# A selective scan with convolution and attention on one core: preparation of steps re-timed, image ends allowed to run over, and a wide last end

## The chip, the cores and the metric

The kernel runs on one core of one Trainium2 chip. The metric is the device time of one execution in microseconds (us). A profiled execution gives a trace of every instruction on each engine: PE (TensorE matmul; PEld is its weight load), DVE (VectorE), ACT (ScalarE), POOL (GpSimd) and SP (SyncE, which here only issues DMAs).

## The reference

The input x is 8 images of 64×64 positions × 96 channels, fp32. Two layers follow, cut here to what matters:

```python
# layer 0:  x = x + ss2d(groupnorm(x))
xh, z = split(x @ in_proj_w.T)                    # 192 + 192 channels
xc = silu(depthwise_conv3x3(xh) + conv_b)
s0, s1 = xc[diag], xc[anti]                       # two walks over the 4096 positions
xs = [s0, s1, s0[::-1], s1[::-1]]                 # four directions
dts, Bs, Cs = split(x_proj_weight @ xs)           # 6 + 16 + 16 rows
delta = softplus(dt_projs_weight @ dts + bias)
h_t = h_{t-1} * exp(delta_t * A) + (delta_t * u_t) * B_t     # per channel and state, 16 states
y_t = sum over states of h_t * C_t;  ys = y + D * xs
y = the four directions put back in place and added
out = (layernorm(y) * ln_w + ln_b) * silu(z) @ out_proj_w.T
# layer 1:  t = t + linear_attention(layernorm(t)) (6 heads);  t = t + ffn(layernorm(t))
# the ffn has 96 -> 384 -> 96 channels, inputs and weights rounded to 5+2 bits, sums to 5+10 bits
```

## The kernel before

**The main loop.** An image is scanned in 16 steps: two passes q (forward directions, then backward), each of 8 chunks of T=512 positions. The two directions of a pass lie together on the 128 partitions, in G=3 groups of channels. Each step has 16 states n, so there are 128 steps m and 2048 iterations i = 16·m + n in `run`. One iteration issues, in this order:

- `decay(i+2)`: three Exp on ACT (L966), from delta;
- `times_b(i+2)`: where FEED[n] is "A", eight scaled copies on ACT (L980) into feedT, from duT and rows. FEED is "DADADADADADAAAAA": n=0, 2, 4, 6, 8 and 10 go the other way, by one pick matmul (L990) and three DVE multiplies (L1005) in `recur`;
- `recur(i)`: three scans on DVE (L1001), of 512 elements each;
- `turn(i+1)`: PE transposes (L988) of feedT into the three feed banks of PSUM;
- `reduce(i-4)`: PE transposes (L1036) of the products into the y banks, where the 16 states are summed;
- `keep(i-1)` and `read(i-1)`: on POOL the carry (L1017) and the product of h and C (L1022);
- `fetch(i+4)`: two DMAs on SP that broadcast a row of C into cc.

PSUM's eight banks are three of feed, three of y and two ("bank") shared by everything else.

**The preparation of a step** is `prologue(m+2)`, started at n=13 of step m. It makes x_proj (L878), rows (L883), their transposes (L888) and x (L891); |dt| in three groups (matmul L901, ACT Abs L903), Exp (L905) and Ln (L908); then four passes on POOL (L912, L913, L915, L917), which together give log(1+e) with a correction of its rounding; then delta in three groups (matmul L920, DVE L922), du on POOL (L929), its transposes (L934) and copies into duT on ACT (L936). `bring(m+2)`, at n=8, loads u, and first finishes side work until that chunk has been walked.

**Side work** is everything that isn't the loop: `measures` (group norm statistics), `front` (norm, convolution L536, silu, image stores L562, and the walk: loads of ut on SP L581, transposes L588), and `tail` (`join` from L614: normalises y, gates it, projects it; `attention`; `layers`: attention's output and the FFN). It is written as generators. Class `Work` advances them in fixed places of an iteration, by a credit of us for each place ("P" for PE three times an iteration, "A" for ACT, "V" for DVE, "G" for POOL). Urgent jobs (prologues) come first. In its alone mode, `finish(enough)`, it runs whatever is there until a condition holds. [...]

During image b, `between(b)` runs the front of image b+1 and then the tail of image b-1. The hand-over is at iteration LAG+1 = 5 of an image:

```python
            if at == LAG + 1 and b:
                work.finish(all_done)
                work.stream(between(b))
```

The measures of image b+2 start in mid-image. Before the loop, image 0's front runs until two chunks are walked, and prologue(0) is finished together with whatever side work is there. After the loop, `end(7)`, the last tail, runs with the feed banks freed, three chunks at a time. The join of a chunk stores t (`at.mid`) and the transposed xaT (`at.turned`) to DRAM, and `layers` loads them.

Of the kernel before, what the change touches and what calls it, by code (L numbers as in the profile page):

```python
# [50 lines left out]
@with_exitstack  # L51
def hybrid_block(ctx, tc, x, out, w):


    nc = tc.nc
    NB = x.shape[0]
    const = ctx.enter_context(tc.tile_pool(name="const", bufs=1))
    dram = ctx.enter_context(tc.tile_pool(name="dram", bufs=4, space=DRAM))
    k = weights(tc, const, dram, w)
    pool = ctx.enter_context(tc.tile_pool(name="scan", bufs=1))  # L60
    psum = ctx.enter_context(tc.tile_pool(name="psum", bufs=1, space=PSUM))
    with tc.manual_schedule():

        k.tables = lambda: nc.scalar.preload_act_table_set("natural_log_exp_and_others")
        run(tc, pool, psum, dram, x, out, k, NB)


def weights(tc, const, dram, w):
# [60 lines left out]
    logs = tile("logs", [P, ND, NJ])  # L129
    turned = tile("turned", [ND * NJ, P])  # L130

    def loads():

        nc.sync.dma_start(out=logs, in_=w["a_logs"])
        for d in range(2):
            for g, a, lo, hi, at in PIECES:
                rows = slice(d * GC + at, d * GC + at + hi - lo)
                for first, n, name in ((0, NR, "w_dt"), (XB, NS, "w_b"), (XC, NS, "w_c")):
                    nc.sync.dma_start(
                        out=k.wx[rows, :, g, first + d * n : first + (d + 1) * n], in_=w[name][lo:hi, a, d::2, :]  # L140
                    )
                nc.sync.dma_start(out=dd[rows, :, g], in_=w["ds"][lo:hi, a, d::2])
                for q in range(2):
                    bias = w["b_step"][lo:hi, 2 * q + d, a : a + 1].rearrange("i o -> o i")
                    nc.sync.dma_start(out=k.ws[2 * NR : 2 * NR + 1, q, g, rows], in_=bias)
                if g:
                    yield SPIN
            for q in range(2):
                nc.sync.dma_start(
                    out=k.ws[d * NR : (d + 1) * NR, q, :, d * GC : (d + 1) * GC],  # L150
                    in_=w["w_step"][:, 2 * q + d, :].rearrange("r (g i) -> r g i", i=GC),
                )


        ps = yield bank(0.2, 3)
        v = view(ps, ND * NJ, P)
        nc.tensor.transpose(v, logs.rearrange("p k j -> p (k j)"), k.ident)
        yield act(0.4)
        nc.scalar.copy(turned, v)
        k.release(ps)  # L160
        rows = dram.tile([ND * NJ, P], F32, tag="logs", name="logs")
        nc.sync.dma_start(out=rows, in_=turned)
        yield SPIN
        for q in range(2):
            for d in range(2):
                for g in range(G):
                    j = (2 * q + d) * NJ + g * (GC // DPT)
                    nc.sync.dma_start(
                        out=k.a_neg[d * GC : (d + 1) * GC, q, g, :],
                        in_=rows[j : j + GC // DPT, :].rearrange("j (i n) -> (j i) n", n=NS),  # L170
                    )
            yield SPIN
# [18 lines left out]
    def layers():  # L191
# [18 lines left out]
        with tc.tile_pool(name="prep", bufs=1, side="right") as prep:  # L210
            w1s = load("w1s", [DM, HID], w["w1"], pool=prep)
            w2s = load("w2s", [P, 3, DM], w["w2"], pool=prep)
            b1s = load("b1s", [P, 3], w["b1"], pool=prep)
            b2s = tile("b2s", [P, 4, DM], pool=prep)
            nc.sync.dma_start(out=b2s, in_=w["b2"].unsqueeze(1).to_broadcast([P, 4, DM]))
            for _ in range(2):
                yield SPIN

            nc.vector.tensor_copy(k.w1q, w1s, saturate=False)
            nc.vector.tensor_copy(k.w2q, w2s, saturate=False)  # L220
            s8 = tile("b1e", [P, 3], F8, prep)
            nc.vector.tensor_copy(s8, b1s, saturate=False)
            nc.vector.tensor_copy(k.b1q, s8)
            s8 = tile("b2e", [P, 4, DM], F8, prep)
            nc.vector.tensor_copy(s8, b2s, saturate=False)
            nc.vector.tensor_copy(k.b2q, s8)
# [38 lines left out]
class Work:  # L265
# [6 lines left out]
    def __init__(self, banks):  # L272
        self.now = 0
        self.alone = False
        self.urgent, self.jobs, self.streams = [], [], []
        self.free = [(b, -9) for b in banks]
        self.kept = []
        self.long = []
        self.credit = dict.fromkeys(self.PLACES, 0.0)
# [40 lines left out]
    def at(self, tag, place=0):  # L320
        gain, most = self.PLACES[tag]
        self.credit[tag] = min(most, self.credit[tag] + gain)
        for j in self.urgent + self.jobs:
            while not j.done and j.tag == tag:
                if j.ready > (self.now, place) and (j.spin or not self.alone):
                    break
                if not self.alone:
                    if self.credit[tag] <= (0.0 if j not in self.urgent else -1.5 if tag == "P" else -99.0):
                        break
                given = None  # L330
                if j.bank:
                    given = self.bank_for(j, place)
                    if given is None:
                        break
                self.credit[tag] -= j.us
                self.proceed(j, given, place)
# [41 lines left out]


# [29 lines left out]
def fetched(nc, pool, x, b, c):  # L409
    xt = pool.tile([P, 4, DM], F32, tag="xt", name="xt", bufs=2)  # L410
# [57 lines left out]
def front(tc, work, x, k, at, b):  # L468
# [8 lines left out]
    with tc.tile_pool(name=f"f1_{b}", bufs=1, **area) as p1, tc.tile_pool(name=f"f2_{b}", bufs=2, **area) as p2:  # L477
# [17 lines left out]
        def norm(c):  # L495

            xt = fetched(nc, p2, x, b, c)
# [104 lines left out]
def tail(tc, work, x, out, k, at, b):  # L602
# [3 lines left out]
    with tc.tile_pool(name=f"t1_{b}", bufs=1, **area) as p1:  # L606
# [3 lines left out]
        with tc.tile_pool(name=f"t2_{b}", bufs=2, **area) as p2:  # L610
# [3 lines left out]
            def join(c):  # L614
                s = slice(4 * c, 4 * c + 4)

                def tile(name, shape, bufs=2):
                    return p2.tile(shape, F32, tag=name, name=name, bufs=bufs)
# [7 lines left out]
                t = tile("t", [P, 4, DM], 3)  # L626
                nc.sync.dma_start(out=t, in_=x[b].rearrange("(t p) c -> p t c", p=P)[:, s, :])
                yield "P", 0.0, 4, False
                while c >= 2 and c - 2 not in joined:
                    yield SPIN  # L630
                gate = tile("gate", [HC, 2, CH])
                nc.sync.dma_start(out=gate, in_=at.gate[:, :, c * CH : (c + 1) * CH])
                st, mv = tile("st", [P, 4, 6]), tile("mv", [P, 4, 2])
                yn = ys[0]
                for j in range(2):
# [21 lines left out]
                yg = tile("yg", [HC, 2, CH])  # L657
# [26 lines left out]
                nc.sync.dma_start(out=at.mid[:, s, :], in_=t)  # L684
# [28 lines left out]
                xaT = ys[1].rearrange("p a c -> p (a c)")[0 : DM + 1, 0:CH]  # L713
# [3 lines left out]
                nc.sync.dma_start(out=at.turned[:, c * CH : (c + 1) * CH], in_=xaT)  # L717
                joined.add(c)

            yield [join(c) for c in range(NCH)], 3  # L720
# [3 lines left out]
        def attention():  # L724
# [14 lines left out]
            kf = yield from small([DM, DM], "kf", vk, k.w_ff)  # L739
# [11 lines left out]
        with tc.tile_pool(name=f"t3_{b}", bufs=3, **area) as p2:  # L751

            def layers(c):
# [5 lines left out]
                xaT = tile("xaT", [DM + 1, CH])  # L759
                nc.sync.dma_start(out=xaT, in_=at.turned[:, c * CH : (c + 1) * CH])  # L760
                t = tile("t", [P, 4, DM])
                nc.sync.dma_start(out=t, in_=at.mid[:, s, :])
# [59 lines left out]
            yield [layers(c) for c in range(NCH)], 3  # L822


def run(tc, pool, psum, dram, x, out, w, NB):
# [9 lines left out]
    nc = tc.nc  # L835
    steps = [
# [26 lines left out]
    def prologue(m):  # L863
# [8 lines left out]
        ps = yield bank(1.0, 0)  # L872
        v = view(ps, P, TB, NX)
        for j in range(TB):
            if j == 2:
                yield pe(0.8)
# [5 lines left out]
        rows = o.rows = tile("rows", [P, TB, NX])  # L882
# [28 lines left out]
        yield gp(3.0)  # L911
        nc.gpsimd.tensor_scalar(f, e, 1.0, 1.0, ALU.mult, ALU.add)  # L912
        nc.gpsimd.tensor_scalar(f, f, -1.0, 1.0, ALU.add, ALU.mult)  # L913
        yield gp(3.4, 1)
        nc.gpsimd.tensor_tensor(e, e, f, ALU.subtract)  # L915
        yield gp(3.4, 1)
        nc.gpsimd.tensor_tensor(delta, delta, e, ALU.add)  # L917
        for g in range(G):
            ps = yield bank(0.85)
# [3 lines left out]
            work.release(ps)  # L923
        o.delta = delta
        yield gp(3.4)
# [4 lines left out]
        for j in range(G):  # L930
            ps = yield bank(0.45)
# [6 lines left out]
        o.duT = duT  # L938
# [85 lines left out]
    def reduce(i, part):  # L1024
# [15 lines left out]
        if q and n in (1, 2, 3) and part == 2:  # L1040
            for j in range(4 * (n - 1), 4 * n):
# [4 lines left out]
                )  # L1046
        if q and n in (8, 9, 10) and part == 2:
# [4 lines left out]
            )  # L1052
        if part == 2:
            hs.pop(i)
# [34 lines left out]

    def between(b):  # L1090
# [5 lines left out]
    def first():  # L1096
# [5 lines left out]
        yield from between(0)  # L1102
# [20 lines left out]
    work.finish(lambda: not work.urgent)  # L1123
# [6 lines left out]
    for tag, at in (("P", 2), ("A", 0), ("P", 2)):  # L1130
        work.now += tag == "A"
        work.at(tag, at)
# [11 lines left out]
    for i in range(total + LAG + 1):  # L1144
        m, n = divmod(i, NS)
        b, at = divmod(i, PER)
        if i < total:
            if at == LAG + 1 and b:
                work.finish(all_done)
                work.stream(between(b))  # L1150
            if at == PER // 2 and b + 2 < NB:
                work.stream(before(b + 2))
            if n == NS - 3 and m + 2 < len(steps):
# [4 lines left out]
        if i + 2 < total:  # L1158
            decay(i + 2)
        work.at("A")  # L1160
        if i + 2 < total:
            times_b(i + 2)
# [19 lines left out]
    work.free += [(f, -9) for f in feed]  # L1182
    work.kept = []
    work.stream(end(NB - 1))
# [78 lines left out]
```

## Time and profile before

| | us |
|---|---|
| median of 3 runs | 12009.75 (12005.47 to 12027.36) |
| the profiled execution | 12015.44 |
| its span | 12013.6, mean granted TensorE clock 0.907 |
| first scan begins | 308.2 |
| last scan ends | 11627.8 |

| of the span | busy us | share |
|---|---|---|
| PE | 9964.7 | 83% |
| DVE | 9683.0 | 81% |
| ACT | 9500.1 | 79% |
| POOL | 9739.2 | 81% |

The largest groups are POOL's product L1022 (7073.5 us, 3454 ns each), DVE's scans L1001 (6502.6 us, 1261 ns), ACT's decays L966 (3976.2 us, 713 ns), PE's transposes L1036 (3806.0 us) and L988 (2746.2 us), and ACT's feedT L980 (3671.1 us, 443 ns). A share of busy time is an average over stages with different limits: the steps with side work beside them take up to 102 us, those without 75.2.

### The profile page before, as it was taken

The page shows a single profiled execution, that of the slowest core. Times are in us where ns is not written, and L with a number is a line of the kernel's source. Part 1 is how long each engine was busy: PE and PEld are TensorE (multiplying, and loading weights), DVE is VectorE, ACT ScalarE, POOL GpSimd, SP SyncE. Part 2 cuts the span into 40 slices and gives each one's busy share as a digit, 9 for nine tenths or more (in the row PEclk, how much of TensorE's full clock was granted, in tenths as well). Part 3 has the DMA queues.
Part 4 walks back from the last instruction along what each step waited for, and adds up shares of the span by engine and source line. Part 5 has one row for each costly group of instructions (what it writes and reads, how often), then busy time and mean ns, then how long its engine had stood idle before and what let it go on. Part 6 is the DMA issues. An engine that isn't in the chain of part 4 may idle for free.

```text
span 12013.6 us, 186895 instructions
## 1 busy us (share of the span) xinstructions
PE 9964.7 (83%) x62805; PEld 8013.1 (67%) x62805; DVE 9683.0 (81%) x11092; ACT 9500.1 (79%) x19843; POOL 9739.2 (81%) x6927
## 2 busy tenths in 40 slices
PE   5888889888898888888898888988889888888875
PEld 4676677666676667766676666766667666666653
DVE  1888988888888888888888888888888878888971
ACT  2888888878887788887888778887788878878862
POOL 0879988889878888788988888878898888889972
PEclk8999999998999989999899999989899998988985
DMA  3234333533335333343334433343333533322331
GB/s 98 84 97 129 100 91 89 136 106 101 88 96 143 98 93 95 107 125 103 91 92 128 116 93 90 95 129 109 96 92 92 134 105 94 105 83 82 99 96 39
DMA packets 1126629, 1213.55 MB, mean 101 GB/s; under 512 B 453061, under 2 KB 732326, under 8 KB 1125670
## 3 DMA queue, kind: packets, MB, share of 16 engines
q1 hardware_dynamic: 1125670, 1201.61, 36.4%
q8 instruction: 499, 8.18, 0.3%
q14 instruction: 460, 3.77, 0.1%
HBM read 877.99 MB, written 323.14 MB: 100 GB/s over the span
## 4 chain that ended last, share of the span: by engine, by line
PE 30%; ACT 20%; DVE 20%; POOL 12%; issue 9%; DMA 4%; SPq 3%; DVEq 0%; POOLq 0%; ACTq 0%
DVE h L1001 13%; ACT feedT L980 8%; PE y L1036 7%; PE feed L988 7%; POOL h L1022 7%; ACT decay L966 6%; DVE feed L1005 4%; PE bank L536 3%; DMA cc<-crow 2%; PE bank L878 2%; SPq L581 2%; POOL delta L917 1%; PE bank L920 1%; PE feed L990 1%; PE bank L901 1%
## 5 line engine op out<-in xcount | busy, mean ns | idle before, releaser
L1022 POOL TENSOR_TENSOR h<-h,cc 128x1536 f32<-128x1536 f32 x2048 | 7073.5, 3454 | 390.0 <-DMA cc<-crow 197.1
L1001 DVE TENSOR_TENSOR_SCAN h<-decay,carry,feed 128x512 f32<-128x512 f32 x5376 | 6502.6, 1261 | 635.1 <-PE feed L988 528.8
L966 ACT ACTIVATE decay<-delta,a_neg 128x512 f32<-128x512 f32 x6144 | 3976.2, 713 | 1287.5 <-DVE h L1001 1281.8
L988 PE MATMUL feed<-ident,feedT 128*128 128x128 f32 x15360 | 2746.2, 303 | 1502.8 <-DVE h L1001 1211.3
L1036 PE MATMUL y<-ident,h 128*128 128x128 f32 x24576 | 3806.0, 290 | 72.2 <-ACT ys L1064 40.2
L980 ACT ACTIVATE feedT<-duT,rows 128x192 f32<-128x192 f32 x10240 | 3671.1, 443 | 4.5 <-PE feed L988 3.9
L1036 PEld LDWEIGHTS y<-ident,h 128*128 128x128 f32 x24576 | 3151.0, 151 | 530.5 <-issue 477.3
L988 PEld LDWEIGHTS feed<-ident,feedT 128*128 128x128 f32 x15360 | 1972.3, 155 | 2121.2 <-DVE h L1001 663.5
L1005 DVE TENSOR_TENSOR feed<-feed,du 128x512 f32<-128x512 f32 x2304 | 1442.1, 686 | 209.7 <-PE feed L990 205.2
L1017 POOL COPY carry<-h 128x3 f32<-128x3 f32 x2048 | 395.7, 193 | 1072.5 <-DVE h L1001 959.6
L1001 DVE TENSOR_TENSOR_SCAN h<-decay,feed 128x512 f32<-128x512 f32 x768 | 883.3, 1201 | 95.5 <-PE feed L988 80.4
L536 PE MATMUL bank<-wf,xp 97*128 97x192 f32 x4266 | 864.6, 334 | 1.2 <-DVE delta L922 1.2
L990 PE MATMUL feed<-x,pick 77*128 77x512 f32 x1536 | 848.6, 635 | 0.6
L536 PEld LDWEIGHTS bank<-wf,xp 97*128 97x128 f32 x4266 | 696.0, 195 | 29.6 <-issue 18.5
L922 DVE SCALAR_TENSOR_TENSOR delta<-bank,delta 128x512 f32<-128x512 f32 x383 | 259.7, 678 | 280.8 <-POOL delta L917 144.7
L929 POOL TENSOR_TENSOR du<-delta,u 128x1536 f32<-128x1536 f32 x128 | 449.6, 3513 | 36.1 <-DVE delta L922 36.1
L920 PE MATMUL bank<-x,ws 13*128 13x512 f32 x766 | 444.9, 661 | 17.6 <-DVE delta L922 17.6
L915 POOL TENSOR_TENSOR e<-e,duT 128x1536 f32<-128x1536 f32 x128 | 441.7, 3451 | 14.5 <-ACT delta L908 14.4
L901 PE MATMUL bank<-x,ws 13*128 13x512 f32 x764 | 434.1, 648 | 15.0 <-ACT x L891 15.0
L917 POOL TENSOR_TENSOR delta<-delta,e 128x1536 f32<-128x1536 f32 x128 | 441.2, 3447 | 0.1
L912 POOL TENSOR_SCALAR duT<-e 128x1536 f32<-128x1536 f32 x128 | 193.9, 1514 | 227.8 <-ACT e L905 227.8
L990 PEld LDWEIGHTS feed<-x,pick 77*128 77x128 f32 x1536 | 261.4, 202 | 153.7 <-issue 97.7
(263 smaller groups left out, 9059.9 us busy)
## 6 DMA issues: line engine op xcount, KB each, us to landing
cc<-crow SPq DMA_DIRECT2D x4096, 128.0 KB
u<-seq SPq DMA_DIRECT2D x256, 384.0 KB
wide<-ys SPq DMA_DIRECT2D x512, 192.0 KB
ut<-image SPq DMA_DIRECT2D x768, 64.0 KB
seq<-us SPq DMA_DIRECT2D x128, 384.0 KB
part<-ys SPq DMA_DIRECT2D x64, 768.0 KB
y<-part SPq DMA_DIRECT2D x64, 768.0 KB
y<-wide SPq DMA_DIRECT2D x256, 192.0 KB
```

What stands on the lines that cost most here:

```text
L536: nc.tensor.matmul(v[:, j, :], flat[:, o : o + P], k.wf[:, i, :], start=(i == 0), stop=(i == 8), skip_group_check=True)
L901: nc.tensor.matmul(ps, w.ws[:, q, g, :], x[0 : 2 * NR + 1, :], start=True, stop=True)
L917: nc.gpsimd.tensor_tensor(delta, delta, e, ALU.add)
L920: nc.tensor.matmul(ps, w.ws[:, q, g, :], x[0 : 2 * NR + 1, :], start=True, stop=True)
L966: nc.scalar.activation(decays[i][:, g, :], made[m].delta[:, g, :], AF.Exp, scale=w.a_neg[:, q, g, n : n + 1])
L980: nc.scalar.activation(f[part], o.duT[part], AF.Copy, scale=scale)
L988: nc.tensor.transpose(feed[g][:, j * P : (j + 1) * P], feeds[i][:, j * G + g, :], w.ident)
L990: nc.tensor.matmul(feed[0], w.pick[:, FEED[:n].count("D"), :], made[m].x, start=True, stop=True)
L1001: nc.vector.tensor_tensor_scan(h[:, g, back], a[:, g, back], feed[g][:, back], init, ALU.mult, ALU.add)
L1005: nc.vector.tensor_tensor(feed[g], feed[0], made[m].du[:, g, :], ALU.mult)
L1022: nc.gpsimd.tensor_tensor(hs[i], hs[i], c.unsqueeze(1).to_broadcast([P, G, T]), ALU.mult)
L1036: nc.tensor.matmul(y[:, j, :], hs[i][:, g, r * P : (r + 1) * P], w.ident, is_transpose=True, start=(n == 0 and j % 4 == 0), stop=(n == NS ...
```

## The change

1. **Room in SBUF.** Two tiles of the weights' preparation move to a pool that is closed after use; the FFN's biases are loaded after its weights are cast, in a second such pool; the scan's pool is opened in `run` and closed before the last tail.
2. **The first step alone.** A new method `hurry` is an alone mode for urgent jobs only. prologue(0) runs so before the loop, then prologue(1) as far as its x. In the loop, `hurry` stands ahead of `decay(i+2)` until delta is there, and ahead of `times_b(i+2)` until duT is.
3. **The prologue.** It starts at n=10 instead of n=13. x_proj comes in four pieces of three matmuls; rows has three buffers; the POOL passes and du are asked for one or two iterations apart; the three groups of delta (`bound`) and of duT (`turned`) become urgent jobs of their own. Urgent PE work stops at a credit of -0.5 instead of -1.5, and the skip and other matmuls of `reduce` take 0.9 from it.
4. **Ends may run over.** The `finish(all_done)` at iteration 5 is dropped: one stream waits for each image to have begun and then runs its `between`.
5. **A wide last end.** The last tail runs eight chunks at once, with all eight PSUM banks; it adds y0 and y1 on DVE (128x768) where the others use PE matmuls (L640) and ACT copies (L647); and t and xaT stay in SBUF. Before it, `finish(all_done)` runs what is left of the tail of image 6.
6. norm's xt has three buffers instead of two.

Counts of instructions, before and after: POOL 6932 and 6932, ACT 19845 and 19829, PE 54999 and 54935, DVE 11094 and 11102, SP 7759 and 7727.

The core of the diff:

```diff
+    def hurry(self, enough):
+        self.alone = self.hurried = True
+        while not enough():
+            self.now += 1
+            for tag, place in (("A", 0), ("V", 0), ("P", 2), ("G", 0)):
+                self.at(tag, place)
+        self.alone = self.hurried = False
...
-                    if self.credit[tag] <= (0.0 if j not in self.urgent else -1.5 if tag == "P" else -99.0):
+                    if self.credit[tag] <= (0.0 if j not in self.urgent else -0.5 if tag == "P" else -99.0):
...
-def tail(tc, work, x, out, k, at, b):
+def tail(tc, work, x, out, k, at, b, last=False):
...
+                if last:
+                    yield dve(2.5)
+                    nc.vector.tensor_tensor(yn, ys[0], ys[1], ALU.add)
+                    for i in range(4):
+                        nc.vector.bn_stats(st[:, i, :], yn[:, i, :])
+                        nc.vector.bn_aggr(mv[:, i, :], st[:, i, :])
+                for j in range(0 if last else 2):
...
-        yield gp(3.0)
+        yield gp(1.5)
         nc.gpsimd.tensor_scalar(f, e, 1.0, 1.0, ALU.mult, ALU.add)
+        yield gp(1.5, 1)
         nc.gpsimd.tensor_scalar(f, f, -1.0, 1.0, ALU.add, ALU.mult)
-        yield gp(3.4, 1)
+        yield gp(3.4, 2)
         nc.gpsimd.tensor_tensor(e, e, f, ALU.subtract)
-        yield gp(3.4, 1)
+        yield gp(3.4, 2)
         nc.gpsimd.tensor_tensor(delta, delta, e, ALU.add)
-        for g in range(G):
-            ps = yield bank(0.85)
+        left = [2 * G]
+
+        def bound(g):
+            ps = yield bank(0.85, 1)
             nc.tensor.matmul(ps, w.ws[:, q, g, :], x[0 : 2 * NR + 1, :], start=True, stop=True)
             yield dve(0.7)
             nc.vector.scalar_tensor_tensor(delta[:, g, :], ps, 0.0, delta[:, g, :], ALU.max, ALU.add)
             work.release(ps)
+            left[0] -= 1
+
+        for g in range(G):
+            work.start(bound(g), urgent=True)
+        yield gp(3.4, 2)
+        while left[0] > G:
+            yield "G", 0.0, -1, False
...
+        for b in range(NB):
+            yield [wait(b)], 1
+            yield from between(b)
...
-    work.finish(lambda: not work.urgent)
+    work.hurry(lambda: not work.urgent)
...
-    for tag, at in (("P", 2), ("A", 0), ("P", 2)):
-        work.now += tag == "A"
-        work.at(tag, at)
+    work.hurry(lambda: hasattr(made[1], "x"))
...
-            if at == LAG + 1 and b:
-                work.finish(all_done)
-                work.stream(between(b))
+            if at == LAG + 1:
+                begun[0] = b
...
-            if n == NS - 3 and m + 2 < len(steps):
+            if n == NS - 6 and m + 2 < len(steps):
                 work.start(prologue(m + 2), urgent=True)
...
         if i + 2 < total:
+            work.hurry(lambda: hasattr(made[(i + 2) // NS], "delta"))
             decay(i + 2)
         work.at("A")
         if i + 2 < total:
+            if FEED[(i + 2) % NS] == "A":
+                work.hurry(lambda: hasattr(made[(i + 2) // NS], "duT"))
             times_b(i + 2)
...
+    work.finish(all_done)
+    scans.close()
...
-    work.stream(end(NB - 1))
+    work.stream(tail(tc, work, x, out, w, image(NB - 1), NB - 1, True))
     work.finish(all_done)
```

## The prediction, made before the result was known

> **What bounds the kernel now.** I read the busy line first, then stretches of the timeline, then the waits. Columns of the stretches: length, busy us and instruction count for each engine, granted TensorE clock, DMA share, GB/s.
>
> ```profile
> PE 9964.7 (83%) x62805; PEld 8013.1 (67%) x62805; DVE 9683.0 (81%) x11092; ACT 9500.1 (79%) x19843; POOL 9739.2 (81%) x6927
> ```
> ```profile
> core 0: us, PE busy (x) PEld busy (x) DVE busy (x) ACT busy (x) POOL busy (x), PEclk, DMA share, GB/s
> ...
> 224.00:308.00 84.00, 34.48 (x152) 23.99 (x151) 8.07 (x12) 20.09 (x32) 13.20 (x5) 0.62 0.47 121
> 1220.00:1522.00 302.00, 257.72 (x1627) 202.09 (x1626) 280.23 (x277) 263.99 (x560) 284.06 (x149) 0.93 0.37 100
> 5180.00:5576.00 396.00, 328.15 (x2198) 267.12 (x2199) 319.87 (x433) 300.43 (x654) 319.09 (x300) 0.95 0.37 104
> 11628.00:11830.00 202.00, 130.60 (x607) 111.34 (x606) 39.18 (x151) 38.62 (x97) 39.08 (x155) 0.67 0.30 77
> 11830.00:12014.00 184.00, 64.06 (x249) 37.90 (x248) 24.96 (x81) 41.35 (x85) 39.74 (x105) 0.50 0.09 28
> ```
>
> No engine is full over the span. Times of the scan (L1001) cut the run in three: the first begins at 308.2 us, the last ends at 11627.8, and the span ends at 12013.6. So: start 308, loop 11,320 (128 steps), end 386. Row 224–308 is the first step's preparation, with DVE at a tenth. Row 1220–1522 is four steps with nothing beside them: 75.5 us each, DVE 93% and POOL 94% busy. Row 5180–5576 is four steps that carry a join: 99 us each, with every engine at 76–83%. By the ends of the scans a whole image takes 1447 us where 16 bare steps take 1206; the 241 us on top split as convolution and front 62.5, walk 20.7, join 94, attention and layers 64. The last two rows are the tail of image 7.
>
> ```profile
> DVE h L1001 <- PE feed L988: 609.2, 479, 9.5
> DVE feed L1005 <- PE feed L990: 205.2, 242, 4.1
> ...
> POOL h L1022 <- DMA cc<-crow: 197.1, 26, 15.1
> ...
> DVE delta L922 <- POOL delta L917: 144.7, 27, 13.6
> DVE delta L922 <- PE bank L920: 126.4, 126, 3.1
> ```
>
> The waits (total, times, longest) say what DVE lacks: feed rows from PE; and, for the step after next, delta, which POOL and PE deliver late: 144.7 + 126.4 = 271 us.
>
> **What the Trainium skill says.** "TensorE: Matmul & The Clock Gate", What's actually happening: an idle array runs cold. The trace agrees: granted clock 0.95 in the loop, 0.62 in the preparation, 0.50 in the last 184 us. The same page, Architectural detail: ACT and DVE execute strictly in order. So a delta that waits on DVE holds the scans behind it, and what I move on ACT counts at its new place. "VectorE: DVE Perf Modes", The TRN2 errata, gives (N+151)/0.96 ns for an fp32 add: 691 ns at 512, while L1005 shows 686; so 768 elements are an estimated 0.96 us.
>
> **The change, part by part**, against the profiled execution of before (12015.44 us; its span 12013.6).
>
> 1. *First step alone: −50.* 224–308 mixes prologue(0) with image 0's walks and measures of image 1 (PE busy 34 of 84). Alone, its chain is matmuls, rows 0.41, x 0.68, Abs 3×0.58, Exp 1.49, Ln 1.56, POOL 1.5+1.5+3.45+3.45+3.5, transposes and copies 3×0.57: 20 us of work, and with hand-overs and cold matmuls some 34. The first scan comes near 258. The 60 walk loads (L581, 0.61 us of SP each) and the measures then run in the loop.
>
> 2. *Wide last end: −21 (−60 to +20).* Before: 386, of which the join takes 202 and the layers 184, three chunks at a time; each round of layers holds about 17 us of reloading t and xaT. After, eight chunks go together, 128 matmuls (L640, 0.33) and 16 copies (L647, 0.48) become 8 adds at 0.96, and nothing is reloaded. But since ends may run over, the layers of image 6 now lie behind the last scan: 8 chunks in threes, about 150. SP issues the loads of the wide join only after the last store of these; 10.75 MB take 57 at an estimated 190 GB/s (the loop's 104 at a DMA share of 0.37 would be 281 when full; two thirds of it). Join and layers in lockstep are bound by POOL's rsqrt and scaling (3.75 per chunk, twice: 60), ACT's identities and FFN (48), and cold matmuls (60): 158. Sum 365.
>
> 3. *Work that changes place in the loop: −31.* One image's layers leave it; five walks and one measure come in, each at its share of the 241 above, in steps that were nearly bare.
>
> 4. *Ends may run over: +88 (+20 to +120).* Before, at the sixth iteration of each image everything left was finished at once, and nearly nothing was. After, side work has no such line, fronts slip (image 1's convolution in steps 4–9, image 5's in 7–13 and those of the last two in 10–14), until `bring` needs a walked chunk that isn't there. By program order that happens twice, in images 5 and 6, step 14, n=8: 57 and 81 convolution matmuls (0.33: 19–27 us), silu and stores, then 36 walk loads (22 us of SP), ahead of the loop's own instructions on PE, ACT and SP. A stall of 55–62 us each, less the 14–18 that the same work costs piecewise. What is late next: cc<-crow behind the walk loads, then POOL's products. Before's own walk burst (n=7 of step 6) shows the form: 36 loads, POOL waiting 13.7, one iteration of 17.5 us instead of 5.
>
> 5. *duT hurried: +40 (0 to +70).* In some 11 steps duT isn't done by n=14, and all that is left is issued at once: POOL e−, delta+, du, about 10 us in a row ahead of its product, 3–6 us lost each time.
>
> 6. *POOL's passes spread, delta bound apart: −60 (−200 to 0).* Two iterations apart, each pass (3.45) falls between products instead of after another. At most the 271 us of delta waits go; two conditions limit it: bare steps already run at 94% of POOL, and PE's part (126.4) only moves to other places.
>
> 7. *Prologue begins at n=10 instead of 13: +80 (0 to +256).* Order puts rows at n=12, x at 13, Abs at 14, 15, 0, where before they stood at 0–4 of the next step. The iterations from n=11 to 15 are all fed by ACT: 8 feedT × 0.443 + 3 decays × 0.713 (some already done ahead) against DVE's 3 × 1.26; a bare step loses 3.8 us there, ACT taking 4.6–4.9 an iteration. Rows, x and two Abs are 2.3 us more in that run; counted fully, 2.0 × 128 = 256. I take under a third: where side work is heavy PE or DVE ends last, and n=0–4 gets the 2.3 back.
>
> 8. *The rest: 0.* x_proj in four pieces and PE's credit (−0.9) move matmuls between iterations in which PE has 10 us a step to spare; if PE's cover were gone, 12 matmuls a step come no later than now. Prep pools hide behind the first loads; norm's third xt covers a load that nothing in the waits above names. Bounds ±20.
>
> Sum −50 −21 −31 +88 +40 −60 +80 = **+46**: 12,061 for the profiled execution. The median of the runs shown, 12009.75, is 5.7 below it, so 12,056.
>
> **The rivals.**
> *A (likeliest, 0.5): slightly slower.* Start and end gain 70–100; flushes, hurries and the moved ACT work take that back. For it: program order shows the slipping fronts plainly, and no sum of the loop's gains is as certain as the 22 us of loads in each flush. 12,056, within 11,990–12,130.
> *B (0.33): faster.* The delta waits go (−200 in place of −60), the flush costs only what runs ahead of DVE's next multiply (+40 in all, since scans with feed already in PSUM go on), and ACT's extra hides (+20): 12,010 −50 −21 −31 +40 +30 −200 +20 = 11,800; with half of that, 11,900. For it: join steps run at 80% of everything, so a smoother order has 16 us a step to win. Against: a delta wait removed often shows as feed wait (609.2) instead.
> *C (0.14): clearly slower, ACT binds the run n=11–15.* The whole 2 us a step is paid: +256 in place of +80, so 12,230. It decides from where ACT's time per A iteration passes the loop's, which in bare steps is already so. Against: only some 15 of 128 steps are bare.
> *D (0.03): the edits cancel within the noise by not doing what they say*, prologue hidden anyway: 12,010.
>
> **How the numbers follow.** About 0.2%, 24 us, is what a measurement of this kernel tells from no change. Faster (under 11,986): all of B but its edge, and a little of A: 0.34. Same: D and A's lower side, 0.14. Slower: 0.52. The likeliest case has 12,056; the range takes in the middle of B and of C, 11,850 to 12,230.
>
> **What would show it.** First scan near 258 us (step 1). Last scan to end near 365, with 150 before the wide join's first add (2). Images 5 and 6 with one iteration or two of over 40 us at step 14 (4). Waits of delta on POOL well under 144.7 (6). Bare steps above 75.2, with PE waiting for feedT at n=12–15 (7). I am wrong if bare steps are at 75 and join steps under 95 (then B), or if bare steps exceed 77 (then C).

## The result: slower by 0.43%, and where the time lies

The changed kernel takes 12,077.94 us (12,045.97 to 12,088.52) where the kernel before takes 12,019.59 over all its runs: a ratio of 1.0043, 95% interval 1.0025 to 1.0061. The forecast was 12,056. The profiled execution has a span of 12,048.3 us, 34.7 more than before.

Cut by the scans (L1052 is now the scan), the profiled executions compare so:

| us | first scan at | loop | from last scan to the end |
|---|---|---|---|
| before | 308.2 | 11,319.6 | 385.8 |
| after | 261.8 | 11,425.8 | 360.7 |
| difference | -46.4 | +106.2 | -25.1 |

The busy line of the page after:

```profile
PE 9956.0 (83%) x62677; PEld 8067.0 (67%) x62677; DVE 9727.1 (81%) x11100; ACT 9468.8 (79%) x19827; POOL 9735.1 (81%) x6927
```

Nothing in it answers the question: each engine does the work that it did before. The stretches of the changed kernel say more (length, busy us and count for each engine, clock, DMA share, GB/s): the preparation of the first step alone, the layers of image 6 behind the last scan, the loads of the wide end, its join and layers, and below them the two long steps of images 5 and 6.

```profile
core 0: us, PE busy (x) PEld busy (x) DVE busy (x) ACT busy (x) POOL busy (x), PEclk, DMA share, GB/s
224.00:262.00 38.00, 21.66 (x55) 12.24 (x53) 3.98 (x7) 14.17 (x25) 13.19 (x5) 0.50 0.08 26
11688.00:11804.00 116.00, 50.39 (x238) 32.32 (x238) 21.10 (x56) 39.59 (x73) 43.85 (x107) 0.55 0.15 43
11804.00:11858.00 54.00, 0.00 (x0) 0.00 (x0) 21.05 (x67) 3.52 (x14) 9.62 (x49) 0.50 1.07 208
11858.00:12048.00 190.00, 119.05 (x674) 85.70 (x674) 48.33 (x174) 65.72 (x150) 65.13 (x208) 0.68 0.03 9
...
8576.00:8728.00 152.00, 115.78 (x665) 95.48 (x662) 78.04 (x82) 86.84 (x166) 69.47 (x37) 0.82 0.43 111
10041.00:10197.00 156.00, 117.41 (x703) 97.72 (x703) 79.60 (x84) 90.36 (x168) 67.09 (x36) 0.87 0.45 114
```

The reader is to see three things. The first row has a step's preparation alone in 38 us, where 84 went before. The end is three stages in a row: 116 of layers on a cold PE (clock 0.55), 54 in which PE does nothing while the loads run at 208 GB/s and DVE adds and measures what has landed (21.05 busy), and 190. The last two rows are single steps of 152 and 156 us, with DVE at half.

By image (from the last scan of one to the last of the next) the loop's 106 split as +71, -21, -3, -14, -47, +35, +32 and +54 for images 0 to 7. So the long steps of images 5 and 6 are only part of it: image 0 and image 7, the first and the last, lose more together than the whole loop does.

The waits of the changed kernel (total, times, longest), against those shown of before:

```profile
DVE h L1052 <- PE feed L1039: 799.6, 522, 33.0
DVE feed L1056 <- PE feed L1041: 322.8, 223, 18.1
ACT rows L920 <- PE bank L915: 245.2, 65, 15.8
POOL h L1073 <- DMA cc<-crow: 185.4, 25, 21.1
PE bank L915 <- DMA u<-seq: 125.0, 21, 16.3
...
DVE delta L962 <- PE bank L960: 71.6, 66, 5.7
DVE delta L962 <- POOL delta L955: 48.5, 7, 35.6
```

and two lines of before that the prediction did not show:

```profile
ACT rows L883 <- PE bank L878: 99.7, 54, 4.9
...
PE bank L878 <- DMA u<-seq: 4.2, 1, 4.2
```

The waits for delta have fallen from 271 to 120 us. What came in their place is the wait for feed (609.2 + 205.2 = 814 before, 1122 now). And there is a wait that was nearly nothing before: x_proj (L915) on PE for u's load, 125.0 for 4.2, and ACT's rows behind x_proj, 245.2 for 99.7. That is where the experiments look.

### The profile page after: what moved, and what is told of

Same layout as the page of the kernel before. It is cut to its first block, busy times and chain, and to the rows that moved or that the text cites. A ratio compares the mean times of both kernels' runs of the same rounds, so it can differ in the third digit from the quotient of the medians.

```text
span 12048.3 us, 186471 instructions
## 1 busy us (share of the span) xinstructions
PE 9956.0 (83%) x62677; PEld 8067.0 (67%) x62677; DVE 9727.1 (81%) x11100; ACT 9468.8 (79%) x19827; POOL 9735.1 (81%) x6927
## 4 chain that ended last, share of the span: by engine, by line
PE 32%; ACT 24%; DVE 18%; POOL 10%; issue 8%; DMA 5%; SPq 3%; DVEq 0%; POOLq 0%; ACTq 0%
DVE h L1052 11%; ACT feedT L1031 9%; PE y L1087 8%; ACT decay L1017 7%; PE feed L1039 7%; POOL h L1073 6%; DVE feed L1056 4%; PE bank L550 3%; PE bank L915 3%; PE bank L960 2%; PE feed L1041 2%; DMA cc<-crow 2%; PE bank L938 1%; DMA u<-seq 1%; SPq L595 1%
## 5 line engine op out<-in xcount | busy, mean ns | idle before, releaser
L1052 DVE TENSOR_TENSOR_SCAN h<-decay,carry,feed 128x512 f32<-128x512 f32 x5376 | 6510.4, 1262 | 853.8 <-PE feed L1039 711.7
L1052 DVE TENSOR_TENSOR_SCAN h<-decay,feed 128x512 f32<-128x512 f32 x768 | 884.8, 1202 | 109.6 <-PE feed L1039 87.9
L915 PE MATMUL bank<-wx,u 128*128 128x77 f32 x3048 | 475.6, 316 | 125.2 <-DMA u<-seq 125.0
L915 PEld LDWEIGHTS bank<-wx,u 128*128 128x128 f32 x3048 | 463.2, 236 | 136.3 <-issue 120.2
```

The source lines that it names most:

```text
L915: nc.tensor.matmul(v[:, j, :], u[:, g, j * P : (j + 1) * P], w.wx[:, q, g, :], start=(g == 0), stop=(g == G - 1))
L1052: nc.vector.tensor_tensor_scan(h[:, g, back], a[:, g, back], feed[g][:, back], init, ALU.mult, ALU.add)
```

## The experiments

In every kernel here the first step is prepared alone and the last end is wide, and the SBUF room and norm's third xt stay. "Old prologue" is the body, the start at n=13 and PE's credits of before; "finished" means that `finish(all_done)` stands at iteration 5 of an image again. A flush is side work that is left over and then run in one go, there or ahead of `bring`; a bare step is one with no side work beside it; the guards are the two calls of `hurry` in the loop. Ratios are to the kernel before, with 95% intervals; loop and end are of the profiled executions, which can lie some 30 us from the median (pool's and the changed kernel's are 32 and 28 below it).

| kernel | prologue | ends | time | ratio | loop | end |
|---|---|---|---|---|---|---|
| clean | old | finished | 11,838 | 0.985 (0.9836 to 0.9863) | 11,307 | 264 |
| over | old | run over | 11,829 | 0.9842 (0.9828 to 0.9855) | 11,304 | 258 |
| pool | old, POOL's passes apart | run over | 11,762 | 0.9783 (0.9766 to 0.9801) | 11,210 | 260 |
| credit | old, new credits | finished | 11,911 | 0.9905 (0.9888 to 0.9921) | 11,395 | 260 |
| early | old, x_proj to x from n=10 | finished | 11,925 | 0.993 (0.9906 to 0.9953) | 11,398 | 262 |
| n10 | old, from n=10 | finished | 12,010 | 0.9995 (0.9986 to 1.0003) | 11,470 | 260 |
| spread | old, x_proj over four iterations | run over | 11,975 | 0.9962 (0.9949 to 0.9975) | 11,343 | 373 |
| newpro | new | finished | 12,245 | 1.0189 (1.0175 to 1.0203) | 11,730 | 254 |
| new13 | new, from n=13 | finished | 12,052 | 1.0024 (1.0015 to 1.0032) | 11,513 | 260 |
| over13 | new, from n=13 | run over | 12,069 | 1.004 (1.0026 to 1.0054) | 11,548 | 264 |
| gain | new, PE's places 1.0 | run over | 12,037 | 1.0016 (1.001 to 1.0023) | 11,426 | 356 |
| unblock | new, urgent jobs hold banks less | run over | 12,083 | 1.0052 (1.0036 to 1.0068) | 11,442 | 362 |

### Prologue or ends: four corners

Kernel *clean* undoes the prologue, the guards and the free-running ends:

```diff
-        for b in range(NB):
-            yield [wait(b)], 1
-            yield from between(b)
+        yield from between(0)
...
-            if at == LAG + 1:
-                begun[0] = b
+            if at == LAG + 1 and b:
+                work.finish(all_done)
+                work.stream(between(b))
...
-            if n == NS - 6 and m + 2 < len(steps):
+            if n == NS - 3 and m + 2 < len(steps):
```

> The prologue, its start at n=13 and PE's credits as before, and everything finished at iteration 5 of an image as before; of the change only the first step alone, the wide last end and the SBUF room stay. Theory (the start and end gain, the rest of the change costs): start -46, end 54 + 190 = 244 instead of 386 because the layers of image 6 are back in the loop, five walks and one measure moved into the loop +33: 12,020 - 46 - 142 + 33 = 11,865. Rival (the walks and measures that now stand beside image 0's steps cost as much as the start gained, and the wide end is no shorter without the layers of image 6 ahead of it): 11,960 or more. Rival (the new prologue or the free-running ends are what gains): this is slower than the kernel with them.

It took 11,838, 182 less than before: -46 at the start, -122 at the end, and the loop no longer (-12), though five walks and a measure moved into it. The start and the wide end alone are a clear gain. What the rest of the change does must be a loss of 240.

Kernel *newpro* undoes the free-running ends only:

> The changed kernel with everything finished again at iteration 5 of an image: ends may not run over, the new prologue stays. Theory as predicted (ACT work moved into n=11 to 15 costs 80, hurries 40, spread POOL passes give 60): 60 slower than the kernel with the old prologue and the same ends, 11,925. Rival B (the delta waits go, the rest hides): 100 or more faster than it, 11,765. Rival C (ACT binds n=11 to 15): 200 or more slower, 12,070.

12,245: with finished ends the new prologue (with its guards) costs 406, twice the least that rival C named. But C's mechanism was one of every step, and here most of the loss stands in one place. Iteration 5 of images 2 to 7 takes 73 us each instead of some 4, about 414 more in all: the `finish` there runs what the image before did not get done. Apart from these iterations images 2 to 6 are even 10 to 20 us shorter than clean's, while image 0, which has no flush, is 65 longer, and image 7 some 30.

Kernel *over* undoes the prologue only (body, n=13, credits):

> The changed kernel with the prologue of before (body, start at n=13, credits): ends run over, first step alone, wide last end. Theory (free-running ends cost: two flushes some 100, and the layers of image 6 moved behind the last scan 116 where they cost some 64 in the loop): 150 slower than the kernel with the old prologue and finished ends, 12,015. Rival (running over costs nothing, the new prologue makes the loss): within 40 of it, 11,905. In the theory no single step is over 140 long if PE's credit, which is larger here, lets the fronts keep up: then only the moved layers remain, +52, 11,917.

11,829, as fast as clean, no step above 103 (before has one of 108, in image 7). So with the old prologue running over costs nothing: a flush needs side work that falls behind. With the new prologue running over is worth 167 (12,245 to 12,078).

### What in the prologue costs

Kernel *n10* is clean with one number changed (and a third buffer of rows, and the guards):

```diff
-            if n == NS - 3 and m + 2 < len(steps):
+            if n == NS - 6 and m + 2 < len(steps):
```

> As the kernel with the old prologue and finished ends, but the old prologue started at n=10 instead of 13 (rows has three buffers, and the guards stand ahead of decay and times_b): the moved ACT work alone, POOL's passes one iteration apart. Theory (ACT's rows, x and Abs in n=11 to 15 cost about 0.6 us a step): 80 slower than it, 11,945. Rival C (paid in full): 256 slower, 12,120. Rival (earlier preparation takes away delta waits and hurries nothing): 50 to 150 faster, 11,765.

+172, between the theory's 80 and rival C's 256. Here too there is a flush, 40 to 42.5 us at iteration 5 of images 2 to 7; images 0 and 7 are 32 and 71 longer than in clean. Kernel *early* parts it, holding back Abs and what follows until the next step:

```diff
         nc.sync.dma_start(out=o.crow, in_=x[XC:NX, :])
+        while m > 1 and clock[0] < NS * (m - 1):
+            yield "G", 0.0, -1, False
```

> The kernel with the old prologue started at n=10 (12,010), but only x_proj, rows, its transposes and x run early; Abs, Exp, Ln and what follows wait until the next step begins, as in the kernel before. It tells PE's and ACT's part of the early start apart. Theory (x_proj before the feed transposes of n=11 and 12, and the rows copy that waits for it ahead of feedT on ACT): bare steps stay at 78 or more with n=11 near 7.4, and the time at 11,960 or more. Rival C (ACT's Abs in the run n=11 to 15): bare steps near 76, and 11,860.

+87 with x_proj, rows and x alone, so about half of n10's loss; the early Abs, Exp, Ln and what follows them make at most the other half. The time lies between the two expectations, the bare steps are as the theory has them: 78.5 instead of 75.2, with n=11 at 8.9. By image, 34 and 61 of the loss stand in images 0 and 7 and next to none in those between, whose flushes of 21 us are made good by shorter steps. The tile view of x_proj's weight loads in one bare step shows the same 24 records (12 matmuls in two passes each) at its two places (min/median/max in ns, then first and last start); clean first:

```profile
L915 PEld LDWEIGHTS bank<-wx,u x24: 191/192/193, 1408.6 to 1411.2; 128*128 128x128 f32 x24
```

and early:

```profile
L915 PEld LDWEIGHTS bank<-wx,u x24: 190/333/337, 1417.1 to 1421.4; 128*128 128x128 f32 x24
```

At n=13 PE is busy with feed transposes, and x_proj takes 2.8 us; at n=10 to 11, after a state that DVE feeds, PE has just been idle (1.9 us in this step, 3.2 in n10's), and the same work takes 4.8, at 333 ns a load. The granted clock over it is 0.55, after 1.00 in the stretch that ends with the idle time (columns as in the stretches above):

```profile
1410.00:1416.00 6.00, 4.38 (x18) 2.10 (x18) 5.89 (x7) 6.00 (x16) 5.84 (x5) 1.00 0.59 148
1417.10:1422.00 4.90, 4.90 (x29) 4.90 (x27) 3.13 (x4) 2.96 (x6) 4.74 (x5) 0.55 0.16 54
```

This x_proj stands between the transposes of two feed groups, so DVE waits 2.7 us for the second. Over the whole run the groups (busy, mean ns, idle before) of clean, n10 and the changed kernel, in this order, say that this is not confined to bare steps:

```profile
L915 PEld LDWEIGHTS bank<-wx,u 128*128 128x128 f32 x3048 | 352.9, 193 | 0.5
```
```profile
L915 PEld LDWEIGHTS bank<-wx,u 128*128 128x128 f32 x3048 | 485.2, 253 | 135.6 <-issue 129.2
L915 PE MATMUL bank<-wx,u 128*128 128x77 f32 x3048 | 492.8, 335 | 130.4 <-DMA u<-seq 130.3
```
```profile
L915 PE MATMUL bank<-wx,u 128*128 128x77 f32 x3048 | 475.6, 316 | 125.2 <-DMA u<-seq 125.0
L915 PEld LDWEIGHTS bank<-wx,u 128*128 128x128 f32 x3048 | 463.2, 236 | 136.3 <-issue 120.2
```

The last columns are the second price: `bring` issues u's load at n=8 as before, and x_proj, now two iterations behind it, waits for it at the head of PE's queue, 125 to 130 us in all, in 16 to 21 of the 128 steps; in early, with the same start, it is 34. In step 9 of image 0 of the changed kernel PE waits 13.2 us for u and DVE 16.7 for the feed behind it, an iteration of 22.5.

What early doesn't tell is how its 87 divide between the slow x_proj and the wait for u: no kernel moved u's load with the start.

Kernel *credit* changes the credits alone:

```diff
-                    if self.credit[tag] <= (0.0 if j not in self.urgent else -1.5 if tag == "P" else -99.0):
+                    if self.credit[tag] <= (0.0 if j not in self.urgent else -0.5 if tag == "P" else -99.0):
...
+            work.credit["P"] -= 0.9
```

> The kernel with the old prologue and finished ends (11,838), with only PE's credits of the change: urgent work stops at -0.5, and the skip and other matmuls take 0.9 each. Theory (the prologue's new body and its early start leave side work over, the credits don't): within 40 of it, 11,860. Rival (the credits, 5.4 of some 41 in a step, leave the side work over that is then flushed at iteration 5): 150 or more slower, 11,990, with iterations of 30 or more at iteration 5 of an image.

+73, between the two expectations, and with the rival's sign, though smaller than it said: iteration 5 of images 2 to 7 takes 26 us. Image 7 is another 15 longer outside its flush.

Kernel *new13* puts newpro's start back to n=13:

> The kernel with the new prologue and finished ends (12,245), but the prologue starts at n=13. Theory (x_proj at n=10 and 11 stands before the feed transposes of the run that ACT feeds, and costs 3.6 a step): bare steps near 75 to 76 again except where duT is hurried, and a time of 12,070 or less. Rival (the new body, with its jobs holding PE's banks, makes the whole loss): within 60 of 12,245. Rival (all of the loss is the early start): 11,840 to 11,880.

-193 from newpro, about halfway to clean, as the theory said: flushes at iteration 5 of 24 us (31 in image 2) instead of 73, bare steps at 75 to 76, but +213 against clean. And n=0 now takes up to 27 us.

### POOL's passes alone

Kernel *pool* is over with the spacing only:

```diff
-        yield gp(3.0)
+        yield gp(1.5)
         nc.gpsimd.tensor_scalar(f, e, 1.0, 1.0, ALU.mult, ALU.add)
+        yield gp(1.5, 1)
...
-        yield gp(3.4, 1)
+        yield gp(3.4, 2)
         nc.gpsimd.tensor_tensor(e, e, f, ALU.subtract)
-        yield gp(3.4, 1)
+        yield gp(3.4, 2)
```

> The kernel with the old prologue and ends that may run over (11,829), with only POOL's softplus passes two iterations apart, started at n=13 as before. As predicted of this part alone: 60 faster, 11,769, delta waits on POOL well under 152. Rival (two iterations later for delta and du, so duT is late and hurried, and side work is held back): 40 or more slower, 11,870.

-67, and with 11,762 the fastest kernel of the study. Its waits, then those of over:

```profile
DVE feed L1043 <- PE feed L1028: 520.5, 305, 14.4
DVE h L1039 <- PE feed L1026: 384.3, 337, 8.8
...
DVE delta L960 <- POOL delta L955: 67.2, 18, 34.7
```
```profile
DVE h L1038 <- PE feed L1025: 592.8, 470, 5.7
DVE feed L1042 <- PE feed L1027: 215.5, 249, 14.3
...
DVE delta L959 <- POOL delta L954: 152.2, 25, 35.7
```

The wait on POOL loses 85; the two feed waits together gain 97 (808 to 905). So the gain doesn't stand in DVE's waits by name. By iteration, n=7 and n=15 get 1.8 and 1.5 us shorter on average and n=0 2.6 longer; each of the images 1 to 6 gets 12 to 25 us shorter. That a late delta also held back what was behind it would fit, but isn't shown.

### The flush, the banks, x_proj in pieces, and the start once more

Kernel *gain* gives PE's places 1.0 instead of 0.85 (the part of the line that changes):

```diff
-"P": (0.85, 1.2)
+"P": (1.0, 1.2)
```

> The changed kernel (12,078), with PE's places for side work given 1.0 us each instead of 0.85. Theory (with the new prologue the side work of an image no longer fits its 16 steps by these credits; what is left over is the flush in images 5 and 6 and the layers of image 6 after the loop): the steps of over 150 go, the end falls from 361 towards 260, the steps in between get longer; 11,905. Rival (engines and not credits bound the steps): within 40 of 12,078.

The two long steps are gone (the longest is 111), and yet the profiled loop has the same 11,425.8 us and the end still has image 6's layers behind it. By the medians the kernel gains 41, a quarter of what the theory said; the profiled executions differ by 10 only, as the changed kernel's was one of its fast ones. So the net price of the two flushes together is small, about 41 if nothing else moved; since the edit gives PE's places more in all iterations, it is not measured alone.

Kernel *unblock* lets an urgent job hold PE's banks only when it is ready:

```diff
-            if any(u.tag == "P" and u.bank for u in self.urgent) or j.bank == "long" and self.long:
+            if any(u.tag == "P" and u.bank and u.ready <= (self.now, place) for u in self.urgent) or j.bank == "long" and self.long:
```

> The changed kernel (12,078), but an urgent job keeps the banks from side work only once it is ready to issue, not while it waits for its iteration. Theory (the many urgent jobs of the new prologue hold side work back, which is left over and flushed in one go): the two steps of over 150 in images 5 and 6 go, about 100 faster, 11,975. Rival (side work is left over because the steps have no room for it): within 30 of 12,078 and the long steps stay.

12,083, with the long steps in place (149 and 161). This theory fell: jobs that wait for their iteration are not what holds side work back.

Kernel *spread* gives each piece of x_proj an iteration of its own, from n=11:

```diff
         for j in range(TB):
-            if j == 2:
-                yield pe(0.8)
+            if j:
+                yield pe(0.7, 1)
```

> The kernel with the old prologue and ends that may run over (11,829), with x_proj in four pieces of three matmuls, each in an iteration of its own, from n=11 on. Theory (x_proj in one piece stands between the feed transposes of two groups: a bare step loses 2.2 at n=14): bare steps near 73.5, and 1 to 2 us a step: 11,640 to 11,740. Rival (its bank is held for four iterations, while duT needs the other, and side work gets none): slower, 11,900 or more.

The rival's time is right: +147. In bare steps n=14 takes 3.9 where it took 5.7, but n=15, n=10 and n=4 to 9 give most of it back (74.8 to 75.9 a step), and fronts slip to steps of 115, 167 and 157 in images 4 to 6, and image 6's layers lie behind the loop (373). That the bank held for four iterations is what keeps side work back, as the rival has it, was not tested apart from the start at n=11.

Kernel *over13* is the changed kernel started at n=13:

> The changed kernel (12,078) with one number put back: the prologue starts at n=13 instead of n=10. Theory (the early start is most of the loss: x_proj at n=10 and 11 on a PE that has cooled down, ahead of the feed transposes): about 190 faster, as between the two kernels with the new prologue and finished ends, 11,890; what is then left to the best kernel (11,762) is PE's credits and the prologue's separate jobs. Rival (with ends that run over the early start costs little, and the loss lies in the credits and jobs): within 60 of 12,078.

12,069: the theory fell. The start put back makes the end 97 shorter (image 6's last store is 54 us ahead of the last scan, where it was 116 behind it), and the loop 122 longer: n=0 takes 9.55 on average instead of 8.30, with single iterations of 23 to 27 at n=0. In the longest of these (27.4 us) the trace has, ahead of the first scan, not only the three duT copies that were late, but the next step's x, Abs, Exp, Ln and POOL's four passes, 10 us in a row on POOL: `hurry` runs every urgent job, not the one alone that is waited for. The changed kernel has the same: its nine longest iterations at n=0 take 15.0 to 19.4 us, where none is over 8.8 before, and in each POOL runs the next step's four passes in a row. It looks like this in the longest (image 0, step 9), on POOL and then on DVE (start, length, what, idle before):

```profile
1013.10 1.47 POOL L949 TENSOR_SCALAR duT<-e 128x1536 f32<-128x1536 f32 x1 [10.52 <-ACT e L942]
1014.66 1.47 POOL L951 TENSOR_SCALAR duT<-duT 128x1536 f32<-128x1536 f32 x1
1016.21 3.43 POOL L953 TENSOR_TENSOR e<-e,duT 128x1536 f32<-128x1536 f32 x1
1019.72 3.44 POOL L955 TENSOR_TENSOR delta<-delta,e 128x1536 f32<-128x1536 f32 x1
...
1023.37 3.44 POOL L1073 TENSOR_TENSOR h<-h,cc 128x1536 f32<-128x1536 f32 x1
```
```profile
1021.02 1.90 DVE L1056 TENSOR_TENSOR feed<-feed,du 128x512 f32<-128x512 f32 x3 [12.51 <-PE feed L1041]
```

Against pool, which has the same start and the same spacing, over13 loses 307. That is the credits, the four pieces and the separate jobs for delta and duT together; of these only the credits were run alone, and with finished ends. If their 73 hold here, some 234 are left to the pieces and the separate jobs. With finished ends a like sum, new13's 213 less 73 for the credits and with pool's 67 added back, leaves 207. Both are estimates that take the parts to add up; how the 307 part among them stays open.

## Why the prediction was right, and where its steps were not

The time, the sign and the two ends held. The loop's sum (+117 from steps 3 to 7) came near the measured +106 by luck: its parts were off in both directions.

1. *First step alone, -50.* Measured -46.4, by the mechanism named: 38 us of preparation alone.
2. *Wide last end, -21.* Measured -25.1. The terms: layers of image 6 at 116 for 150, loads 54 for 57 (208 GB/s for 190), join and layers 190 for 158. The last was too low: PE is busy for 119 there, at a clock of 0.68, where 60 were put down, ACT for 66 instead of 48 and POOL for 65 instead of 60. (The three figures of the prediction add up to 168, not to the 158 that it wrote.) The estimate of 0.96 us for an add of 768 elements held: 0.958. The step also shows what the layers cost there: without them, in clean, the end is 264.
3. *Moved work, -31.* Not isolated. That clean's loop is 12 shorter than before's, with all walks in it, says that the +33 for walks and measures was too much.
4. *Ends may run over, +88.* The place was right to the iteration (n=8 and 9 of step 14 in images 5 and 6), and so was the form. In the chain of waits of that stretch (start, length, what) PE's convolution comes first, then ACT's silu and the image stores, and SP's walk loads last:

```profile
8629.37 4.10 PE bank L550 x24
...
8637.27 3.12 PE bank L550 x19
8640.38 12.16 issue
...
8663.60 2.22 DMA image<-pre
8666.10 0.62 SPq L595
8666.77 0.61 SPq L595
```

("issue" is time for which the profile names no wait.) The stalls are 63 and 73 above the usual 5 to 6 an iteration, for 55 to 62. But the price was wrong. The step charged 14 to 18 for the same work done piecewise; in *gain*, where it is done so, the time falls by 41 (give or take some 20) and not by 88. And the cause was misnamed: *over* runs its ends over without one flush and as fast as *clean*, and with the new prologue running over gains 167. So the step's +88 has the wrong sign in one pair and is nothing in the other.
5. *duT hurried, +40.* Not isolated. n=14 and 15, where the guards stand, are no longer than before (4.49 and 5.60, for 4.71 and 6.54). The hurries show at n=0, where what is issued behind them is used: it takes 8.30 for 6.33, about 250 us over the 127 steps after the first. Some 94 of these are in the nine iterations of 15 us and more, where 11 steps were forecast to lose 3 to 6 each. The rest of the 250 is not all theirs: *pool*, with a gain, has 8.90 at n=0.
6. *POOL's passes apart, -60.* *pool* measured -67, at the start of before. Of the two conditions that were to limit it, the second held: the feed waits took the wait's place in the table.
7. *Start at n=10, +80.* A mis-sized term. With finished ends it measured +172 (*n10*) and +193 (new13 to newpro), and *early* showed that half isn't ACT's: x_proj on PE was costed at nothing, as moved between iterations with PE to spare (step 8). PE had time to spare there, and x_proj ran cold (clock 0.55); and u's load, which was not moved, became a wait. The prediction does not ask when u lands. But in the changed kernel itself the start is worth 9 us (*over13*), which the noise covers: of the 122 that the loop loses when it is put back, the end gives back 97 (both of the profiled executions).
8. *The rest, 0.* The larger miss. The credits cost 73 with finished ends, where ±20 was allowed. The four pieces and the separate jobs for delta and duT, which no step charged anything for, come to an estimated 207 to 234 by what is left of new13 and over13; neither was run alone. (*spread* does not price the pieces: there they stand an iteration apart, and from n=11.)

Of the rivals, D is out. C's sign was met (two bare steps of image 0 take 79.0 and 79.2, n=11 7.4 of it), above the 77 that the prediction named as C's sign; but C's time was not met, and *early* puts the stall on PE's x_proj rather than on ACT. B's gain exists (*pool*), and was paid over by the rest of the prologue. As a sum over single parts: over 11,829, passes -67, early start +172, credits +73 give 12,007, and 71 are left to 12,078. That sum can't be trusted: two of its parts were measured with finished ends, and in the changed kernel the start's number alone is worth 9, so that what the parts do to each other is as large as they are.

## What to carry to other kernels

Judge a bundle by undoing its parts in pairs: here two edits were worth -182 and a third -67, and the rest took back all of it and 58 more. When you prepare something earlier, ask what its first instruction then waits for and what stands behind it on that engine: a load that had been issued 20 us ahead in a bare step of clean had 11 in n10, enough there, but in 16 other steps it was awaited at the head of PE's queue. Where something is hurried, look at what else the hurry issues: here the next step's preparation ran with it, ahead of the scans. Hurrying the one job alone was not tried. And where work is fitted into credits, look at when the last of it is finished against the end of the loop: a schedule may keep its step times and fall behind by a whole stage.

## What the runs showed of the hardware that was not expected

PE's speed changes within one step of the loop, not only between stages. The Trainium skill, "TensorE: Matmul & The Clock Gate", What's actually happening, has an idle array run cold; I had applied that to the start and the end. In the loop, x_proj's weight loads take 192 ns at n=13 and 333 at n=10 to 11: the trace agrees, with a granted clock of 0.55 over x_proj in early, after a gap of 1.9 us on PE and 1.00 in the six us before that gap. Over 300 ns are 1.5% of them in before and in clean, 23% in early, 31% in the changed kernel and 43% in n10. They are not what makes the changed kernel slow by themselves: over13 has 8% of them and takes 12,069.
